# The softplus step of a selective-scan kernel: where its last sums and its product run

## The chip, the cores and the metric

The kernel runs on one core of one Trainium2 chip. The metric is device time in microseconds, from one launch to the end; the time before is the median of three runs. The engines are named as in the profile: PE is TensorE (matrix products), DVE is VectorE, ACT is ScalarE, POOL is GpSimd, SP only issues DMAs.

## The reference, cut to what matters

A model of four layers works on four images of 96 channels and 64 x 64 pixels. Layer 0 is a selective scan in four directions over 192 inner channels with 16 states each; layer 1 is a deformable convolution; layers 2 and 3 are a Fourier filter, a linear attention and two quantised feed-forward blocks. The change lies in layer 0, where the step size `delta` is a softplus:

```python
dts = jnp.einsum('bkrl,kdr->bkdl', dts, dt_w)
...
delta = jax.nn.softplus(dts + delta_bias[None, :, :, None])
...
dA = jnp.exp(d_t[..., None] * A)
h = dA * h + (d_t * u_t)[..., None] * b_t[:, :, None, :]
y = jnp.einsum('bkdn,bkn->bkd', h, c_t)
```

So for each direction, channel and pixel the kernel needs `delta` and `delta * u`, before the scan reaches that pixel.

## The kernel before, in words

**The scan** (`Layer0.scan`) is the backbone of the program. It has 1536 units (4 images, 4 directions, 4 pieces of 1024 pixels, 24 groups of 8 channels times 16 states on 128 partitions). A unit loads `delta` for its channels, each row repeated 16 times, into `da` (`fetch`, L911, a DMA issued by ScalarE); ScalarE takes the exponential (`decay`, L932, two units ahead); TensorE spreads `delta * u` over the states into the PSUM tile `db` (`inflow`, L938, one unit ahead); VectorE multiplies `db` by B in place (`enter`, L952) and runs the recurrence (`recur`, L960); GpSimd keeps the last column (L967) and multiplies by C (`weigh`, L969); TensorE sums over the states into `py` (`total`, L988), which ScalarE copies out (`settle`, L999).

**Beside the scan** two streams of other work are emitted: one makes the inputs of layer 0 image by image (`before`: normalisation, convolution at L691, and the chains below) and afterwards layers 2 and 3; the other runs what follows the scan of layer 0 and then layer 1 with its gathers (L1301, L1312, L1331, L1352). Each is a generator that yields steps, and each step says what it should take of each engine: `cost(pe=..., dve=..., act=..., pool=...)`. A planner (`Clock`, `pipe`, `Stream`) adds these up at the time of building and emits a step when its engines have room and its input is due. The order of instructions on every engine is the order of emission. The numbers in `cost` are the planner's estimates, not measurements. A step can also say how many of the three shared PSUM banks its chain holds (`holds`), and take or free a token for a buffer (`takes`, `frees`); a chain waits where a token is missing.

**The chains** (`Layer0.steps`) make `delta` and `delta * u` for 512 pixels on 128 partitions; there are 192 of them, 48 for each image, up to five at a time in `pipe`. A chain's stages are, in order:

- TensorE multiplies the projected inputs by `dt_w` into the PSUM tile `pd` (L769). ScalarE takes `ex = exp(-|pd|)` (L771, L772), `lw = ln(ex + 1)` (L774) and `w1 = ex + 1` (L775).
- VectorE takes `w1 - 1 - ex`, which is what was lost in rounding `ex + 1` (L778). GpSimd subtracts it from `lw` (L780). VectorE takes `rl = max(pd, 0) + lw`, which is `delta` (L782).
- VectorE multiplies `rl` by `u` into `ex` (L785, where the direction runs down the columns and `u` is read with a stride; L791 elsewhere). SP writes `rl` to DRAM (L794).
- ScalarE and TensorE split `ex` into three bf16 parts (L798 to L808; `minus` is minus the identity in bf16), which SP writes to DRAM (L812). `inflow` reads them back.

The tiles `lw` and `w1` exist once, `rl` and `du` twice, `ex` three times, as do the shared PSUM banks.

Of the kernel before, what the change touches and what calls it, by code (L numbers as in the profile page):

```python
# [10 lines left out]
BF16 = mybir.dt.bfloat16  # L11
# [4 lines left out]
ALU = mybir.AluOpType  # L16
# [9 lines left out]
CH = 512  # L26
# [157 lines left out]
def cost(pe=0.0, dve=0.0, act=0.0, pool=0.0, **more):  # L184
    return Step((pe, dve, act, pool), **more)


def wait(us=0.0, **more):

    return Step((0.0,) * 4, us, **more)  # L190
# [75 lines left out]
class Chain:  # L266
    def __init__(self, steps, ready):
        self.steps, self.ready = steps, ready
        self.done, self.holds, self.new, self.takes = 0, 0, True, []
        self.kind = steps.gi_code  # L270


def pipe(net, chains, width, every=0, **tiles):
# [5 lines left out]
    while True:  # L279
        if more and len(active) < width:  # L280
            steps = next(chains, None)
            if steps is None:
                more = False
            else:
                active.append(Chain(steps, clock.now()))
                continue
# [252 lines left out]
class Layer0:  # L539
# [211 lines left out]
    def steps(self, b, ks, j, us, dtw, sm, xdbl):  # L751

        net = self.net
        nc = net.nc
        cs = slice(j * CH, (j + 1) * CH)
        tk = f"{b}_{j}_" + "".join(str(k) for k in ks)
        both = len(ks) == 2

        def tile_of(name, bufs):
            return sm.tile([128, CH], F32, name=f"{name}{tk}", tag=name, bufs=bufs)  # L760

        yield wait(new=True, takes="ex lw")


        pd = net.mm(f"pd{tk}")
        for k in ks:
            q = k % 2
            o, m = (pd[64 * q : 64 * q + 64], slice(128, DI)) if both else (pd, slice(0, 128))
            nc.tensor.matmul(o, lhsT=dtw[:, k, m], rhs=xdbl[q, j], start=True, stop=True)  # L769
        ex = tile_of("ex", 3)  # L770
        nc.scalar.activation(ex, pd, AF.Abs)  # L771
        nc.scalar.activation(ex, ex, AF.Exp, scale=-1.0)  # L772
        lw, w1 = tile_of("lw", 1), tile_of("w1", 1)
        nc.scalar.activation(lw, ex, AF.Ln, bias=net.one)  # L774
        nc.scalar.activation(w1, ex, AF.Identity, bias=net.one)  # L775
        yield cost(pe=2.2 if both else 1.1, act=2.7, holds=1, takes="rl")
        rl = tile_of("rl", 2)
        nc.vector.scalar_tensor_tensor(w1, w1, -1.0, ex, ALU.add, ALU.subtract)  # L778
        yield cost(dve=0.7, holds=1)
        nc.gpsimd.tensor_sub(lw, lw, w1)  # L780
        yield cost(pool=1.3, holds=1)
        nc.vector.scalar_tensor_tensor(rl, pd, 0.0, lw, ALU.max, ALU.add)  # L782
        yield cost(dve=0.7, frees="lw")
        if not both and ks[0] % 2:
            nc.vector.tensor_mul(  # L785
                ex.rearrange("p (w h) -> p w h", h=H),
                rl.rearrange("p (w h) -> p w h", h=H),
                us[1][:, j * NR : (j + 1) * NR, :],
            )
        else:  # L790
            nc.vector.tensor_mul(ex, rl, us[2 if both else 0][:, cs])  # L791
        parts = ((0, 64, ks[0], 128), (64, 128, ks[1], 128)) if both else ((0, 128, ks[0], 0),)
        for p0, p1, k, c0 in parts:
            nc.sync.dma_start(self.de_d[b][k][c0 : c0 + p1 - p0, cs], rl[p0:p1])  # L794
        yield cost(dve=0.7, takes="du", frees="rl")

        du = sm.tile([128, 3, CH], BF16, name=f"du{tk}", tag="du", bufs=2)
        nc.scalar.copy(du[:, 0, :], ex)  # L798
        yield cost(act=0.6, new=True)
        pr = net.mm(f"pr{tk}")  # L800
        nc.tensor.matmul(pr, lhsT=net.ident, rhs=ex, start=True, stop=False)  # L801
        nc.tensor.matmul(pr, lhsT=self.minus, rhs=du[:, 0, :], start=False, stop=True)
        nc.scalar.copy(du[:, 1, :], pr)
        yield cost(pe=1.5, act=0.6, holds=1, frees="ex")
        nc.tensor.matmul(
            pr, lhsT=self.minus, rhs=du[:, 1, :], start=False, stop=True, skip_group_check=True
        )
        nc.scalar.copy(du[:, 2, :], pr)  # L808
        yield cost(pe=0.4, act=0.6)
        for p0, p1, k, c0 in parts:  # L810
            dst = self.du_d[b][k][:, c0 : c0 + p1 - p0, cs]
            nc.sync.dma_start(dst.rearrange("s c t -> c s t"), du[p0:p1])  # L812
        self.ready.update((b, k, both, j) for k in ks)
        yield wait(frees="du")
# [974 lines left out]
```

## Time and profile before

| what | value |
|---|---|
| median of three runs | 9014.61 us (9012.24 to 9038.34) |
| profiled execution, first to last instruction (span) | 8965.3 us |
| median of the runs less that span | 49.3 us (the profiled execution's own whole time is not given) |
| granted TensorE clock, mean | 0.807 |
| VectorE busy | 6689.3 us, 4995 instructions |
| TensorE busy | 6639.1 us, 31960 products |
| GpSimd busy | 5561.5 us, 4307 instructions |
| ScalarE busy | 5244.1 us, 10214 instructions |

The profile is one execution of the program, recorded by the hardware. A row of a group reads: line, engine, operation, output<-inputs by the program's names, shapes, count; then busy time in us and the mean of one in ns; then the time for which the engine stood idle just before such an instruction, and what ended that idle time. A row of a table of windows gives, for a stretch of time, the busy time of each engine with its number of instructions, the granted clock, the share of the DMA engines and the GB/s. A row of one line's view gives minimum, median and maximum in ns.

### The profile page before, as it was taken

The numbers are of one execution on the slowest core, as the hardware profiler recorded it, in microseconds if no ns is written. First come the engines' busy times: TensorE is split into PE (matmuls) and PEld (weight loads), VectorE is DVE, ScalarE is ACT, GpSimd is POOL, SyncE is SP. The second block draws the span as 40 slices with busy tenths as digits, with TensorE's granted clock in tenths as the row PEclk, the third lists the DMA queues.
The fourth block names the chain that finished last, engine by engine and source line by source line (L and its number), as shares of the span: only waits on it lengthen the run. The fifth ranks groups of instructions, "written<-read, shape, count | busy, mean of one in ns | idle before, by whom it ended". The sixth has DMA issues, their size and how long they took to land.

```text
span 8965.3 us, 97776 instructions
## 1 busy us (share of the span) xinstructions
PE 6639.1 (74%) x31960; PEld 2926.8 (33%) x31960; DVE 6689.3 (75%) x4995; ACT 5244.1 (58%) x10214; POOL 5561.5 (62%) x4307
## 2 busy tenths in 40 slices
PE   6675967687767678777667888776888777766687
PEld 2111311122222233312223554122455322454373
DVE  0498889987889987788898887898887889223414
ACT  4564656555567767755566665545666665267623
POOL 0365657666668888766688887667888876245200
PEclk8776977798778889877778888787898887867798
DMA  1476777767778888877788888667888876434120
GB/s 51 133 205 173 193 191 220 198 183 181 189 202 231 235 224 228 204 199 194 200 230 219 233 218 213 160 177 193 215 229 222 216 188 156 104 108 131 57 62 12
DMA packets 776001, 1608.49 MB, mean 179 GB/s; under 512 B 247810, under 2 KB 339358, under 8 KB 773383
## 3 DMA queue, kind: packets, MB, share of 16 engines
q10 hardware_dynamic: 244224, 843.17, 36.4%
q1 hardware_dynamic: 457542, 532.51, 22.0%
q0 software_dynamic: 73728, 226.57, 9.6%
q8 instruction: 257, 4.21, 0.2%
q14 instruction: 250, 2.04, 0.1%
HBM read 1345.62 MB, written 256.29 MB: 179 GB/s over the span
## 4 chain that ended last, share of the span: by engine, by line
PE 35%; DVE 27%; DMA 15%; ACT 10%; issue 7%; POOL 2%; SPq 2%; ACTq 1%; another core or an unknown queue 0%; DVEq 0%; POOLq 0%
DVE hh L960 13%; DVE db L952 7%; DMA du<-du 5%; PE pc L691 4%; PE py L988 4%; ACT g L1312 4%; PE ps L1331 3%; PE db L938 3%; PE f L1425 3%; DMA da<-de 2%; PE pd L1347 2%; POOL hh L969 1%; DMA bc<-bcd 1%; ACT da L932 1%; PE h L1466 1%
## 5 line engine op out<-in xcount | busy, mean ns | idle before, releaser
L969 POOL TENSOR_TENSOR hh<-hh,bc 128x1024 f32<-128x1024 f32 x1536 | 3658.6, 2384 | 351.9 <-DVE hh L960 244.2
L960 DVE TENSOR_TENSOR_SCAN hh<-da,st,db 128x1024 f32<-128x1024 f32 x1152 | 2701.1, 2345 | 229.9 <-PE py L988 86.1
L952 DVE TENSOR_TENSOR db<-db,bc 128x1024 f32<-128x1024 f32 x1536 | 1863.4, 1213 | 523.2 <-PE db L938 517.9
L932 ACT ACTIVATE da<-da,w_al 128x1024 f32<-128x1024 f32 x1536 | 1741.5, 1146 | 641.0 <-DMA da<-de 287.2
L938 PE MATMUL db<-du,rep 96*128 96x512 bf16 x3072 | 1101.2, 447 | 824.6 <-DVE hh L960 764.5
L1301 POOL DMA_INDIRECT g<-table,idx x1152 | 1151.2, 999 | 546.3 <-issue 195.7
L1312 ACT ACTIVATE g<-g,wt 128x96 f32<-128x96 f32 x4608 | 1282.6, 365 | 146.8 <-DMA du<-du 37.3
L988 PE MATMUL py<-hh,w_fold 128*32 128x512 f32 x6144 | 1055.2, 760 | 24.2 <-POOL hh L969 10.7
L960 DVE TENSOR_TENSOR_SCAN hh<-da,db 128x1024 f32<-128x1024 f32 x384 | 877.3, 2285 | 71.9 <-PE py L988 22.1
L1331 PE MATMUL ps<-w_ident,g 128*96 128x128 f32 x3744 | 682.8, 322 | 300.6 <-ACT g L1312 142.7
L938 PEld LDWEIGHTS <-rep 96*128 96x128 bf16 x3072 | 284.3, 107 | 1772.3 <-issue 1139.0
L780 POOL TENSOR_TENSOR lw<-lw,w 128x512 f32<-128x512 f32 x192 | 244.3, 1273 | 820.9 <-DVE w L778 808.7
L1331 PEld LDWEIGHTS ps<-w_ident,g 128*96 128x96 f32 x3744 | 483.2, 142 | 655.0 <-ACT g L1312 255.2
L967 POOL COPY st<-hh 128x1 f32<-128x1 f32 x1152 | 233.3, 202 | 696.0 <-DVE hh L960 637.4
L691 PE MATMUL pc<-pad,wc 96*128 96x512 f32 x1152 | 548.4, 616 | 53.4 <-DMA wc<-wc_d 46.8
L1339 ACT COPY st<-ps 96x384 f32<-96x384 f32 x384 | 180.2, 472 | 395.5 <-PE ps L1331 301.6
L801 PE MATMUL pr<-ex,w_ident 128*128 128x512 f32 x384 | 281.5, 823 | 173.0 <-DVE ex L791 89.8
L778 DVE SCALAR_TENSOR_TENSOR w<-w,ex 128x512 f32<-128x512 f32 x192 | 159.4, 830 | 285.7 <-ACT w L775 285.6
L1318 DVE TENSOR_TENSOR g<-g 128x576 f32<-128x576 f32 x96 | 72.9, 759 | 390.0 <-ACT g L1312 360.5
L691 PEld LDWEIGHTS pc<-pad,wc 96*128 96x128 f32 x1152 | 217.1, 195 | 336.4 <-issue 305.3
L988 PEld LDWEIGHTS py<-hh,w_fold 128*32 128x32 f32 x6144 | 153.9, 122 | 511.0 <-issue 384.4
L769 PE MATMUL pd<-xd,w_dtw 103*64 103x512 f32 (+1 forms) x512 | 267.1, 800 | 66.5 <-DVE rl L782 27.5
(249 smaller groups left out, 8899.5 us busy)
## 6 DMA issues: line engine op xcount, KB each, us to landing
da<-de ACTq DMA_DIRECT2D x1536, 512.0 KB
du<-du SPq DMA_DIRECT2D x512, 192.0 KB
bc<-bcd SPq DMA_DIRECT2D x128, 512.0 KB
du<-du SPq DMA_DIRECT2D x128, 384.0 KB
y<-yb SPq DMA_DIRECT2D x384, 128.0 KB
de<-rl SPq DMA_DIRECT2D x128, 256.0 KB
m<-in_dft SPq DMA_DIRECT2D x128, 256.0 KB
ad<-y ACTq DMA_DIRECT2D x192, 128.0 KB
```

What stands on the lines that cost most here:

```text
L691: nc.tensor.matmul(pp, lhsT=wc[:, q, g * 128 : (g + 1) * 128], rhs=pad[:, r0 + dy : r0 + dy + NR, dx : dx + W], start=(q == 0), stop=(q == 8),
L801: nc.tensor.matmul(pr, lhsT=net.ident, rhs=ex, start=True, stop=False)
L932: self.net.nc.scalar.activation(u.da, u.da, AF.Exp, scale=self.al[:, a : a + 1])
L938: self.net.nc.tensor.matmul(db[:, h, :], lhsT=self.rep[:96, u.s % 4, :], rhs=u.du[u.s // 4][:, h * CH : (h + 1) * CH], start=True, stop=True,)
L952: self.net.nc.vector.tensor_mul(u.db, u.db, u.bc[:, 0, :])
L960: nc.vector.tensor_tensor_scan(u.along(u.hh), u.along(u.da), u.along(u.db), first, ALU.mult, ALU.add)
L969: self.net.nc.gpsimd.tensor_mul(u.hh, u.hh, u.bc[:, 1, :])
L988: nc.tensor.matmul(py[p0 : p0 + 32], lhsT=self.fold[:, u.i, :], rhs=hc[:, h * CH : (h + 1) * CH], start=u.sums["add"] is None and u.i == 0 ...
L1301: nc.gpsimd.indirect_dma_start(out=g[:, k, :], out_offset=None, in_=self.tables[b % 2], in_offset=bass.IndirectOffsetOnAxis(ap=idx[:, n : ...
L1312: nc.scalar.activation(pixel, pixel, AF.Identity, scale=wt[:, n, c : c + 1])
L1331: nc.tensor.matmul(pt[:, k, :], lhsT=g[:, k, c * C : (c + 1) * C], rhs=net.ident, is_transpose=True, start=(c == 0), stop=(c == corners - 1),)
L1425: nc.tensor.matmul(pt[64 * part : 64 * part + 64, c, :], lhsT=d[:, :, c0 + c], rhs=matrix[:, 64 * part : 64 * part + 64], start=True, stop ...
```

## The change

The subtraction of what was lost in rounding leaves GpSimd. VectorE writes it as a bf16 tile `lost`, forms `max(pd, 0) + lw` in place in the PSUM tile, TensorE adds minus `lost` to it there, and ScalarE copies the finished `delta` to `rl`. The product with `u` goes from VectorE to GpSimd. The planner's costs and the tokens of the steps are changed with it: the chain has one step fewer, `rl` is taken one step later, and the bank is held for two steps where it was held for three.

```diff
-        yield cost(pe=2.2 if both else 1.1, act=2.7, holds=1, takes="rl")
+        yield cost(pe=2.2 if both else 1.1, act=2.7, holds=1)
+
+        lost = sm.tile([128, CH], BF16, name=f"lost{tk}", tag="lost", bufs=1)
+        nc.vector.scalar_tensor_tensor(lost, w1, -1.0, ex, ALU.add, ALU.subtract)
+        nc.vector.scalar_tensor_tensor(pd, pd, 0.0, lw, ALU.max, ALU.add)
+        yield cost(dve=1.5, holds=1, takes="rl")
         rl = tile_of("rl", 2)
-        nc.vector.scalar_tensor_tensor(w1, w1, -1.0, ex, ALU.add, ALU.subtract)
-        yield cost(dve=0.7, holds=1)
-        nc.gpsimd.tensor_sub(lw, lw, w1)
-        yield cost(pool=1.3, holds=1)
-        nc.vector.scalar_tensor_tensor(rl, pd, 0.0, lw, ALU.max, ALU.add)
-        yield cost(dve=0.7, frees="lw")
+        nc.tensor.matmul(pd, lhsT=self.minus, rhs=lost, start=False, stop=True, skip_group_check=True)
+        nc.scalar.copy(rl, pd)
+        yield cost(pe=0.4, act=0.6, frees="lw")
         if not both and ks[0] % 2:
-            nc.vector.tensor_mul(
+            nc.gpsimd.tensor_mul(
                 ex.rearrange("p (w h) -> p w h", h=H),
                 rl.rearrange("p (w h) -> p w h", h=H),
                 us[1][:, j * NR : (j + 1) * NR, :],
             )
         else:
-            nc.vector.tensor_mul(ex, rl, us[2 if both else 0][:, cs])
+            nc.gpsimd.tensor_mul(ex, rl, us[2 if both else 0][:, cs])
         parts = ((0, 64, ks[0], 128), (64, 128, ks[1], 128)) if both else ((0, 128, ks[0], 0),)
         for p0, p1, k, c0 in parts:
             nc.sync.dma_start(self.de_d[b][k][c0 : c0 + p1 - p0, cs], rl[p0:p1])
-        yield cost(dve=0.7, takes="du", frees="rl")
+        yield cost(pool=1.3, takes="du", frees="rl")
```

## The prediction

> **What bounds the kernel now.** I read the page first: no engine is busy for more than 75% of the span, but the slices show that the average hides two stages.
>
> ```profile
> PE 6639.1 (74%) x31960; PEld 2926.8 (33%) x31960; DVE 6689.3 (75%) x4995; ACT 5244.1 (58%) x10214; POOL 5561.5 (62%) x4307
> ...
> DVE  0498889987889987788898887898887889223414
> ```
>
> VectorE is at eight or nine tenths from slice 3 to slice 34 (about 350 to 7640 us, the scan) and low before and after. Next, the groups: what the scan needs of each engine for one of its 1536 units.
>
> ```profile
> L969 POOL TENSOR_TENSOR hh<-hh,bc 128x1024 f32<-128x1024 f32 x1536 | 3658.6, 2384 | 351.9 <-DVE hh L960 244.2
> L960 DVE TENSOR_TENSOR_SCAN hh<-da,st,db 128x1024 f32<-128x1024 f32 x1152 | 2701.1, 2345 | 229.9 <-PE py L988 86.1
> L952 DVE TENSOR_TENSOR db<-db,bc 128x1024 f32<-128x1024 f32 x1536 | 1863.4, 1213 | 523.2 <-PE db L938 517.9
> L780 POOL TENSOR_TENSOR lw<-lw,w 128x512 f32<-128x512 f32 x192 | 244.3, 1273 | 820.9 <-DVE w L778 808.7
> ```
>
> A unit costs VectorE 2.33 + 1.21 = 3.54 us and GpSimd 2.38 + 0.2 = 2.6 us; everything else on VectorE comes on top. The changed code (`steps`, 192 chains) runs in four waves, one for each image. I took a table of windows over them, then one stretch without chains:
>
> ```profile
> core 0: us, PE busy (x) PEld busy (x) DVE busy (x) ACT busy (x) POOL busy (x), PEclk, DMA share, GB/s
> 354.20:715.00 360.80, 254.34 (x708) 67.18 (x708) 323.73 (x254) 239.18 (x351) 233.69 (x177) 0.78 0.68 195
> 1157.00:1680.00 523.00, 362.84 (x1151) 91.51 (x1149) 494.13 (x362) 329.26 (x469) 339.61 (x229) 0.77 0.78 211
> 2201.00:3160.00 959.00, 671.80 (x2599) 237.27 (x2601) 857.36 (x589) 613.31 (x1193) 713.48 (x549) 0.77 0.79 213
> 3781.00:4745.00 964.00, 682.29 (x2393) 217.20 (x2394) 840.76 (x597) 569.79 (x1001) 678.75 (x512) 0.77 0.77 205
> ...
> 4860.00:5200.00 340.00, 277.90 (x2165) 172.35 (x2163) 288.50 (x182) 213.52 (x495) 290.15 (x230) 0.89 0.89 230
> ```
>
> In the waves VectorE is 87 to 94% busy, all others 59 to 74%. The same windows of the scan line alone hold 71, 110, 200 and 190 units: 5.08, 4.75, 4.80 and 5.07 us each. The last window has 80 units, 4.25 us each, with VectorE at 85%: that pace is my floor, set there by GpSimd and DMA. So the waves are bound by VectorE, and work taken off it there shortens the scan.
>
> Then the rows of the chain itself (by form, and the lines' minimum, median, maximum):
>
> ```profile
> L785 DVE TENSOR_TENSOR ex<-rl,xa 128x512 f32<-128x512 f32 x64 | 109.7, 1714 | 2.2
> L791 DVE TENSOR_TENSOR ex<-rl,xa 128x512 f32<-128x512 f32 x64 | 77.5, 1211 | 1.8
> L791 DVE TENSOR_TENSOR ex<-rl,xc 128x512 f32<-128x512 f32 x64 | 63.8, 998 | 2.1
> L782 DVE SCALAR_TENSOR_TENSOR rl<-pd,lw 128x512 f32<-128x512 f32 x192 | 130.3, 679 | 27.6 <-POOL lw L780 21.8 <-DMA de<-rl 5.8
> L805 PE MATMUL pr<-du,minus 128*128 128x512 bf16 x192 | 86.9, 453 | 30.2 <-ACT du L803 30.1
> L999 ACT COPY yb<-py 128x512 f32<-128x512 f32 x192 | 110.2, 574 | 117.4 <-DVE hh L960 37.4 <-DMA du<-du 20.8 <-PE py L988 10.5
> ```
>
> ```profile
> L791 DVE TENSOR_TENSOR ex<-rl,xa x64: 674/692/5339, 305.1 to 4740.5; 128x512 f32<-128x512 f32 x64
> ...
> L782 DVE SCALAR_TENSOR_TENSOR rl<-pd,lw x192: 655/680/694, 279.3 to 4739.8; 128x512 f32<-128x512 f32 x192
> ```
>
> The reader is to see that the product takes 0.69 us at the median but 1.2 us in the mean, while the step before it, with one operand in PSUM, never exceeds 0.694.
>
> **What the skill says.** The Trainium skill, "SBUF — State Buffer", Who interferes with whom: a VectorE instruction with two SBUF inputs contends with a GpSimd one that reads SBUF, and the later one waits for the whole of the other. The trace agrees: see L791 against L782. "GPSIMD Engine Reference", Elementwise: two-input work is about half as fast there; L780's 1273 ns against 680 agrees. "PSUM — Partial Sum Buffer", the four PSUM rules: GpSimd cannot touch PSUM, hence the ScalarE copy before the moved product; and VectorE's write leaves the bits by which a product without a start flag adds, so the product adds to what VectorE left. No run yet shows that last part.
>
> **The change part by part** (192 chains).
> VectorE: the products L785 and L791 go: 109.7 + 77.5 + 63.8 = 251.0 us. By the windows 7.6 of this lies before the first unit, where VectorE idles and nothing is won; 243.4 lies inside the scan. L778 becomes `lost`, same two f32 inputs, bf16 out: 0.83 us as now. It may inherit lock waits that the product met: from −0.15 (none left) to +0.4 us (what L791 loses on average), −29 to +77 us; I take 0, since its operands and place are as before. L782 writes in place in PSUM: L952 does so in 1.213 us for 1024, which less 512 columns at 0.96 GHz ("VectorE: DVE Perf Modes", Specifications; an estimate) leaves 0.68, as now; bounds ±10 us.
> GpSimd: 192 subtractions go (244.3 us), 192 products come: 128 plain at 1.27, 64 strided at 1.52 (L1052 reads a strided operand in 1518 ns at the median): 260 us. The 16 us more hide under VectorE (GpSimd is at 65 to 74% in the waves); uncovered, they would cost 16.
> TensorE: one bf16 product and its weight load, 192 x (0.45 + 0.11) = 108 us. ScalarE: 192 copies at 0.574 = 110 us. Over the waves' 2807 us that is 4% each: TensorE from 70 to 74%, ScalarE from 62 to 66%, plus its 571 issues of `da` loads at 0.52 us, 11%. Both stay under VectorE.
> Queues: the DMAs of `rl` (L794) stay as many, on SP, in the same place; they now wait for ScalarE's copy in place of VectorE. On TensorE the new product waits for two VectorE instructions; behind it stand the `db` products of the next units. On ScalarE the copy waits for that product; behind it stand the exponentials of `da`, issued two units ahead (VectorE waits for them only 24.8 us in all). On GpSimd the product waits for the copy; behind it stands `hh`, which TensorE needs three units later. The order is planned so that a step is emitted once its input is due, so I expect waits, but short ones.
> The planner sees 1.5 us of VectorE work for a chain where it saw 2.1, one step fewer, and `lw` free without the GpSimd stage between, so chains may follow one another faster and the stream of later stages comes forward.
>
> Sum: without new waits the waves run at 4.54, 4.18, 4.45 and 4.71 us a unit; only the second falls under the floor, (4.25 − 4.18) x 110 = 8 us lost. VectorE now waits in the waves for `db` 57 + 32 + 55 = 144 us; with TensorE fuller and one more wait in its queue I add a third, 45 us. 243 − 8 − 45 = 190 us. The tail after the scan: two strands end 69 us apart (the last `xo` of image 3 at 8444, the last FFN row of image 2 at 8513, then image 3 alone): if the later one comes forward, up to 69 us more; I take 0. Span 8965 − 190 = 8775; the median of the runs lies 49.3 us above this span, so about 8825.
>
> **The rivals.** *Slower: TensorE becomes the bound.* Now TensorE idles before L801 for VectorE's product 193.4 + 96.2 us (with the weight loads), 128 times, 2.26 us each. From GpSimd that product comes 0.58 us later, and up to one `hh` (2.38) after that; with the new wait in front, each chain could hold the in-order queue, `db` comes late and VectorE idles. It decides from 235/192 = 1.22 us of new idle for each chain; at 1.7 us, 326 − 235 = 91 us slower, 9106. For it: VectorE's largest wait is already for `db`, 518 us. Against: TensorE waits for the scan before `db` 764 us, so it has slack of its own.
> *No change: another pace.* If GpSimd or DMA set the waves' pace as they set the floor, what VectorE saves turns into its idle time: 9015. Against: waves one and two run slower than the floor with DMA at 0.68 and 0.78.
> *It doesn't do what it says:* the added operations are all real; what may differ is the emitted order, every later stage being planned anew. That is worth tens of us either way and is in the range.
>
> **Numbers.** VectorE relief 0.68 (8825; its own range 8690 to 8960), no change 0.10, TensorE 0.22. Range 8690 to 9060. Within 0.3% (27 us) is about what a measurement of this kernel can't tell from no change.
>
> **What would show it.** Right: VectorE about 250 us less busy and 4803 instructions; waves at 4.2 to 4.7 us a unit with VectorE still near 90%; scan ending near 7450. Wrong: VectorE's wait for `db` well above 518 us, TensorE's or its weight loads' waits on the new `pd` product or on `ex` above 400 us (TensorE); equal scan end with more VectorE idle and no such waits (other pace); `lost` at 1.2 us (the lock wait only moved).

## The result, and the profile after

The changed kernel took **8932.76 us** in the median (8907.99 to 8966.76) against 9009.08 (8959.19 to 9038.34) for the kernel before on the same chip. The ratio of the runs, 0.9931 [0.9916, 0.9947] (95% interval), is 62 us (48 to 76); the two medians lie 76 us apart. The direction was right; the gain was about a third of the 190 us that were forecast.

The profiled execution took 8943.91 us as a whole with a span of 8942.1, so 1.8 us lie around a span. The span of before that the prediction used therefore belonged to an execution of 8967.1 us, 42 below that kernel's median. The two spans lie only 23 us apart where the medians lie 76 apart: what these traces say of *where* the time went is good to some 50 us, and the ratios carry the verdicts below. Where in the program the 62 us were won, the traces don't show.

The page of the changed kernel, busy time and slices:

```profile
PE 6647.8 (74%) x32152; PEld 2943.2 (33%) x32152; DVE 6549.9 (73%) x4803; ACT 5334.2 (60%) x10406; POOL 5560.8 (62%) x4307
...
DVE  0488889886888877788888787998887978323314
```

VectorE has the 4803 instructions that were foretold, but it is only 139.4 us less busy (6689.3 − 6549.9), not 250. The page of before has this row for the subtraction:

```profile
L778 DVE SCALAR_TENSOR_TENSOR w<-w,ex 128x512 f32<-128x512 f32 x192 | 159.4, 830 | 285.7 <-ACT w L775 285.6
```

The groups of the changed kernel's page say where the rest is:

```profile
L971 POOL TENSOR_TENSOR hh<-hh,bc 128x1024 f32<-128x1024 f32 x1536 | 3638.2, 2371 | 366.3 <-DVE hh L962 257.2
L962 DVE TENSOR_TENSOR_SCAN hh<-da,st,db 128x1024 f32<-128x1024 f32 x1152 | 2700.9, 2345 | 267.0 <-PE py L990 108.2
L954 DVE TENSOR_TENSOR db<-db,bc 128x1024 f32<-128x1024 f32 x1536 | 1864.2, 1214 | 608.0 <-PE db L940 592.6
...
L779 DVE SCALAR_TENSOR_TENSOR lost<-w,ex 128x512 bf16<-128x512 f32 x192 | 252.1, 1313 | 319.1 <-ACT w L775 318.8
L787 POOL TENSOR_TENSOR ex<-rl,xa 128x512 f32<-128x512 f32 x64 | 98.6, 1540 | 551.9 <-ACT rl L784 549.2
```

`lost` (L779) takes 1313 ns in the mean where the same subtraction took 830 before: 192 x 0.483 = 93 us. And VectorE's wait for `db` rose from 517.9 to 592.6 us. The views of the chain's lines (minimum, median and maximum in ns):

```profile
L779 DVE SCALAR_TENSOR_TENSOR lost<-w,ex x192: 665/836/5655, 277.6 to 4663.1; 128x512 bf16<-128x512 f32 x192
...
L780 DVE SCALAR_TENSOR_TENSOR pd<-pd,lw x192: 681/686/695, 278.2 to 4663.7; 128x512 f32<-128x512 f32 x192
...
L783 PE MATMUL pd<-lost,minus x192: 376/380/634, 279.0 to 4670.4; 128*128 128x512 bf16 x192
```

The step with one operand in PSUM (`pd`, L780) lies between 681 and 695 ns in all 192 cases. The one with two operands in SBUF (`lost`, L779) starts at 665 and goes to 5655. Before, 26 of the 192 subtractions took over 0.9 us (the trace, instruction by instruction); now 94 do. Each of these 26 and 94 ends 0.54 to 0.56 us after a GpSimd instruction ended. One of the long ones, in the changed kernel's timeline (start and duration in us, engine, line):

```profile
4457.64 4.69 POOL L971 TENSOR_TENSOR hh<-hh,bc 128x1024 f32<-128x1024 f32 x2
...
4458.29 4.60 DVE L779 SCALAR_TENSOR_TENSOR lost<-w,ex 128x512 bf16<-128x512 f32 x1
...
4462.81 0.69 DVE L780 SCALAR_TENSOR_TENSOR pd<-pd,lw 128x512 f32<-128x512 f32 x1
```

GpSimd runs two multiplications back to back until 4462.33; `lost`, which starts while the first runs, ends at 4462.89, 0.56 us after the second. It counts as busy all that time. It is a wait of the kind that the prediction read off L791, now on another instruction.

The same windows as before:

```profile
core 0: us, PE busy (x) PEld busy (x) DVE busy (x) ACT busy (x) POOL busy (x), PEclk, DMA share, GB/s
354.20:715.00 360.80, 258.08 (x730) 69.26 (x731) 298.14 (x212) 256.87 (x385) 221.73 (x173) 0.80 0.68 193
1157.00:1680.00 523.00, 368.72 (x1211) 95.38 (x1204) 471.36 (x319) 346.82 (x503) 339.95 (x230) 0.80 0.79 213
2201.00:3160.00 959.00, 676.36 (x2675) 241.19 (x2668) 825.42 (x547) 637.66 (x1249) 723.17 (x557) 0.79 0.81 217
3781.00:4745.00 964.00, 683.38 (x2456) 210.75 (x2455) 821.36 (x560) 595.75 (x1032) 684.23 (x515) 0.79 0.80 210
```

VectorE went from 87–94% to 83–90%, and the windows hold 70, 115, 200 and 196 units where they held 71, 110, 200 and 190: 581 for 571. VectorE got room and filled only part of it. The granted clock in these windows is 0.79 to 0.80, where it was 0.77 to 0.78. From the first scan instruction to the last the scan takes 7288 us here and 7268 in a second trace (`e9_after_again`); in two traces of the kernel before it took 7283 and 7303. After the first two waves, with the same 96 chains done, VectorE has spent 62 us less beside the scan than before (326 to 264 us), and yet the first 384 units take as long as before, 1805 us.

### The profile page after: what moved, and what is told of

Same layout as the page of the kernel before. It is cut to its first block, busy times and chain, and to the rows that moved or that the text cites. A ratio compares the mean times of both kernels' runs of the same rounds, so it can differ in the third digit from the quotient of the medians.

```text
span 8942.1 us, 98509 instructions
## 1 busy us (share of the span) xinstructions
PE 6647.8 (74%) x32152; PEld 2943.2 (33%) x32152; DVE 6549.9 (73%) x4803; ACT 5334.2 (60%) x10406; POOL 5560.8 (62%) x4307
## 4 chain that ended last, share of the span: by engine, by line
PE 34%; DVE 23%; DMA 17%; ACT 11%; issue 8%; POOL 3%; ACTq 1%; SPq 1%; another core or an unknown queue 0%; DVEq 0%; POOLq 0%
DVE hh L962 12%; DVE db L954 6%; DMA du<-du 5%; PE pc L691 4%; ACT g L1314 4%; PE py L990 4%; PE ps L1333 3%; PE db L940 3%; PE f L1427 3%; DMA da<-de 3%; PE pd L1349 2%; ACT da L934 2%; POOL hh L971 1%; PE py L985 1%; DMA bc<-bcd 1%
## 5 line engine op out<-in xcount | busy, mean ns | idle before, releaser
L954 DVE TENSOR_TENSOR db<-db,bc 128x1024 f32<-128x1024 f32 x1536 | 1864.2, 1214 | 608.0 <-PE db L940 592.6
L940 PE MATMUL db<-du,rep 96*128 96x512 bf16 x3072 | 1074.9, 437 | 819.3 <-DVE hh L962 775.2
L990 PE MATMUL py<-hh,w_fold 128*32 128x512 f32 x6144 | 1034.9, 746 | 17.3 <-ACT yb L1001 5.9
L779 DVE SCALAR_TENSOR_TENSOR lost<-w,ex 128x512 bf16<-128x512 f32 x192 | 252.1, 1313 | 319.1 <-ACT w L775 318.8
L787 POOL TENSOR_TENSOR ex<-rl,xa 128x512 f32<-128x512 f32 x64 | 98.6, 1540 | 551.9 <-ACT rl L784 549.2
L1349 PE MATMUL pd<-st,wdc 96*128 96x256 f32 x1152 | 309.9, 417 | 4.4 <-ACT st L1341 4.4
L803 PE MATMUL pr<-ex,w_ident 128*128 128x512 f32 x384 | 270.8, 795 | 44.5 <-POOL ex L787 17.3
```

The costliest lines, as they stand in the source:

```text
L940: self.net.nc.tensor.matmul(db[:, h, :], lhsT=self.rep[:96, u.s % 4, :], rhs=u.du[u.s // 4][:, h * CH : (h + 1) * CH], start=True, stop=True,)
L954: self.net.nc.vector.tensor_mul(u.db, u.db, u.bc[:, 0, :])
L990: nc.tensor.matmul(py[p0 : p0 + 32], lhsT=self.fold[:, u.i, :], rhs=hc[:, h * CH : (h + 1) * CH], start=u.sums["add"] is None and u.i == 0 ...
L1349: nc.tensor.matmul(po, lhsT=wdc[:, k, :], rhs=st[:, k, :], start=(k == 0), stop=(k == 8))
```

## The experiments

Theory: VectorE's busy time in the waves is worth time, and the wait at the port that VectorE shares with GpSimd moved from the product to `lost`. Rivals: TensorE became the bound; another pace (GpSimd, DMA) holds the scan; the order of emission, planned anew, makes the difference. A further one, the granted clock, is taken up behind the table. The ratios below are to the kernel before, on the chip of that run.

**The product made short, before's code otherwise** (`e1_product_short`):

```diff
-            nc.vector.tensor_mul(ex.rearrange(...), rl.rearrange(...), us[1][:, j * NR : (j + 1) * NR, :])
+            nc.vector.tensor_mul(ex[:, :8], rl[:, :8], us[1][:, j * NR, :8])
...
-            nc.vector.tensor_mul(ex, rl, us[2 if both else 0][:, cs])
+            nc.vector.tensor_mul(ex[:, :8], rl[:, :8], us[2 if both else 0][:, j * CH : j * CH + 8])
```

> The kernel before with its order unchanged, the product of delta and u on VectorE cut to 8 of 512 columns (the rest of ex stays as it was, so delta times u is left out). Theory V (VectorE's time sets the pace of the waves): VectorE is about 200 to 240 us less busy and the time falls by 130 to 240 us, ratio 0.974 to 0.986. Theory O (the pace comes from the order in which the engines must serve one another, TensorE above all): VectorE's idle time grows by most of what it saves, the time falls by less than 70 us, ratio above 0.992. Theory L (the wait for the shared port only moves): the remaining step with two SBUF inputs, L778, grows from 0.83 to about 1.2 us; under V alone it stays at 0.83.

Measured: 0.9922 [0.9895, 0.9948]. `delta * u` is left out here but for these columns. The views of the two product lines of this kernel:

```profile
L785 DVE TENSOR_TENSOR ex<-rl,xa x64: 158/173/4461, 283.2 to 4594.3; 128x8 f32<-128x8 f32 x64
...
L787 DVE TENSOR_TENSOR ex<-rl,xc x64: 153/168/3024, 285.3 to 4615.9; 128x8 f32<-128x8 f32 x64
L787 DVE TENSOR_TENSOR ex<-rl,xa x64: 151/168/4849, 304.2 to 4677.4; 128x8 f32<-128x8 f32 x64
```

Eight columns take 0.17 us at the median, yet the three groups hold 50.1 + 48.3 + 32.3 = 130.7 us, 0.68 us each: three quarters of that is waiting. Of the 251 us that the prediction took off VectorE, about 100 were not work at all. L778 kept its 0.82 us here: the short product still does the waiting.

**`lost` with an operand in PSUM, the change otherwise** (`e2_lost_no_lock`; `lost` is made of `pd` and `w1` here):

```diff
-        nc.vector.scalar_tensor_tensor(lost, w1, -1.0, ex, ALU.add, ALU.subtract)
+        nc.vector.scalar_tensor_tensor(lost, pd, -1.0, w1, ALU.add, ALU.subtract)
```

> The changed kernel with its order unchanged, but the step lost reads pd in PSUM in place of ex, so that it has one SBUF input (what was lost in rounding is then not what is subtracted: delta is wrong by this). Theory L: the step falls from 1.31 to 0.68 us, VectorE is about 120 us less busy. Theory V: the time falls by 60 to 120 us below the changed kernel, ratio to before 0.978 to 0.986. Theory O: it stays within 30 us of the changed kernel, ratio 0.989 to 0.995.

Measured: 0.9843 [0.9817, 0.9868]. Its groups by form:

```profile
L780 DVE SCALAR_TENSOR_TENSOR pd<-pd,lw 128x512 f32<-128x512 f32 x192 | 132.4, 690 | 0.0
L779 DVE SCALAR_TENSOR_TENSOR lost<-pd,w 128x512 bf16<-128x512 f32 x192 | 130.8, 681 | 326.1 <-ACT w L775 325.9
```

Only the operands differ, one of them now in PSUM, and 1313 ns become 681: the extra 121 us were the wait at the port. The end moves by 0.9 points (about 80 us) with them. What is taken off is then not the rounding, so the result is not that of the change.

**The product on GpSimd alone** (`e3_product_pool`, before with `nc.gpsimd.tensor_mul` at L785 and L791 and the step's cost as `pool=1.3`) and **the sums in PSUM alone** (`e4_psum_only`, the change with `nc.vector.tensor_mul` and `dve=0.7`):

> The kernel before with only the product moved to GpSimd (and its planned cost with it); the step size is finished as before. VectorE 251 us less busy in the product, GpSimd 260 us more. Theory V: ratio 0.985 to 0.993, with L778 at about 1.2 us (L). Theory O: 0.995 to 1.005, the two GpSimd stages in each chain giving back what VectorE saves.

> The changed kernel with the product back on VectorE (and its planned cost with it): only the finish in PSUM is left of the change. Theory V: VectorE is as busy as before, so ratio 0.997 to 1.003. Theory O: if the gain came from the chain's shorter way (no GpSimd stage between two VectorE steps, lw free sooner, the stream of later stages further ahead at the scan's end), the ratio is that of the whole change, 0.990 to 0.995.

Measured: 1.0033 [1.002, 1.0045] and 1.0098 [1.0073, 1.0123]. Neither half helps. In both the subtraction waits, by form (`e3`, then `e4`):

```profile
L778 DVE SCALAR_TENSOR_TENSOR w<-w,ex 128x512 f32<-128x512 f32 x192 | 221.0, 1151 | 310.4 <-ACT w L775 310.1
```

```profile
L779 DVE SCALAR_TENSOR_TENSOR lost<-w,ex 128x512 bf16<-128x512 f32 x192 | 282.2, 1470 | 279.3 <-ACT w L775 279.2
```

The first is the unchanged subtraction at 1151 ns. The scan shortened to 7184 us, but the chain passes GpSimd twice, the last product of the last wave ended at 4922 us where it was 4742, and the stream behind came late: 7224 TensorE products were left after the scan where before left 6916, and the tail took 1472 us, not 1328. In the second, product and `lost` both wait (1470 ns for `lost`, 1.47 to 1.73 us for the products), and VectorE is 131 us *busier* than before.

Set side by side with before (830 ns, 26 of 192 over 0.9 us) and the change (1313 ns, 94), the two halves narrow down why `lost` waits. Either half alone brings the wait: the product off VectorE (`e3`, 1151 ns, 83 of 192), or the subtraction off GpSimd with the product still on VectorE (`e4`, 1470 ns, 102). So `lost` does not wait only because the product is gone. The trace of before shows what else may have kept its subtraction short: GpSimd stood idle until L778 was done in 159 of the 192 chains, 808.7 us in all, since its own step L780 needs the result. A GpSimd instruction other than an indirect DMA was running at the start of L778 in 30 chains, at the start of `lost` in 104. That this is the reason in `e4` and in the change is argued; `e3` keeps L780 and waits all the same, with 192 products more on GpSimd.

**The kernel before once more** (`e5_before_again`) and **the changed kernel once more** (`e9_after_again`), for a second trace of each:

> The kernel before, unchanged, for a second trace: the first trace of before is of an execution of 8967 us, 42 us under the median of its runs, so the two traces that are compared differ by less than the two medians. Theory H (about half of the time taken off VectorE reaches the end): a more usual execution shows its scan ending 20 to 50 us later than 7637, with the same busy time on VectorE, so that the change's scan is shorter after all. Otherwise the scan ends at 7637 plus or minus 15 and the change gained only in the tail.

> The changed kernel, unchanged, for a second trace on the chip of its companions. Two traces of before have scans of 7283 and 7304 us and tails of 1328 and 1287 us (the tail differs from chip to chip); the one trace of the changed kernel has 7288 and 1294. Theory Q (the scan hardly shortens, since what VectorE saves is paid back on the way through TensorE and ScalarE): the scan is again 7270 to 7310. Otherwise, if that trace was an unlucky one, 7200 to 7260.

8947.71 us beside a median of 8948.48; and 0.9919 [0.9894, 0.9944], VectorE 6557.8 us, `lost` 1368 ns in the mean. The scans of these traces are among those given above.

**`lost` on GpSimd** (`e6_lost_pool`, with one more ScalarE step so that a plain subtraction does):

```diff
+        nc.scalar.activation(w1, w1, AF.Identity, bias=net.neg)
...
-        nc.vector.scalar_tensor_tensor(lost, w1, -1.0, ex, ALU.add, ALU.subtract)
+        nc.gpsimd.tensor_sub(lost, w1, ex)
```

> The changed kernel with its order unchanged, but lost made on GpSimd: ScalarE takes 1 from w1 first, then GpSimd subtracts ex (the result is the same). VectorE loses its last step with two SBUF inputs in the chains: 252 us less busy than in the changed kernel. Theory H: half of this reaches the end, 110 to 140 us below the changed kernel, ratio to before 0.976 to 0.980. Rival W (the chains' way through GpSimd's queue is what counts, as where the product alone was moved): the waves end later than 4660 us, the tail grows, ratio 0.988 to 1.000.

Measured: 1.0006 [0.9991, 1.0021], with VectorE 375 us less busy. Its waits say what became of them:

```profile
DVE db L957 <- PE db L943: 771.0, 313, 23.1
...
DVE hh L965 <- PE py L993: 184.1, 134, 7.0
```

VectorE is free of the wait at the port in the chains and waits for TensorE instead. GpSimd carries 5772.6 us here, 211 more than before.

**Dose on VectorE** (`e7_vector_dose`: `e2` with both VectorE steps on 8 columns, which the product L783 then reads over and over) and **dose on TensorE** (`e8_tensor_dose`: `e2` without the two products L803 of a chain):

```diff
-        nc.vector.scalar_tensor_tensor(pd, pd, 0.0, lw, ALU.max, ALU.add)
+        nc.vector.scalar_tensor_tensor(pd[:, :8], pd[:, :8], 0.0, lw[:, :8], ALU.max, ALU.add)
```

```diff
-        nc.tensor.matmul(pr, lhsT=net.ident, rhs=ex, start=True, stop=False)
-        nc.tensor.matmul(pr, lhsT=self.minus, rhs=du[:, 0, :], start=False, stop=True)
+        nc.tensor.matmul(pr, lhsT=self.minus, rhs=du[:, 0, :], start=True, stop=True)
```

> e2_lost_no_lock with its order unchanged and both VectorE steps of a chain cut to 8 of 512 columns (delta is left out for the rest): VectorE about 200 us less busy than in e2. Theory H (a constant share of about 0.55): 110 us below e2, ratio 0.970 to 0.974. Theory F (VectorE is no longer what bounds the waves by then): less than 50 us below e2, ratio 0.979 to 0.985. Theory V (VectorE alone bounds the waves): 180 to 200 us below e2, 0.962 to 0.965.

> e2_lost_no_lock with its order unchanged and the two f32 products of ident and ex taken out of each chain (delta times u then misses this part): TensorE about 270 us less busy. If TensorE shares the bound with VectorE, since what VectorE waits for is db from TensorE, the time falls by 80 to 150 us below e2, ratio 0.968 to 0.976. If only VectorE and its lock count, it stays within 30 us of e2, ratio 0.981 to 0.988.

Measured: 0.9776 [0.9752, 0.98] and 0.9868 [0.9844, 0.9891]. VectorE's 182 us less (6418.2 to 6236.5) gave another 0.7 points. TensorE's 384 products fewer gave nothing that can be told from `e2`. But the dose was small: they had taken 258.5 us of TensorE in `e2`, and TensorE is only 97 us less busy (6617.4 to 6520.4), because the other products took longer, at a granted clock of 0.796 where `e2` has 0.814:

```profile
L990 PE MATMUL py<-hh,w_fold 128*32 128x512 f32 x6144 | 1023.9, 740 | 24.6 <-ACT yb L1001 8.3
```

```profile
L989 PE MATMUL py<-hh,w_fold 128*32 128x512 f32 x6144 | 1057.3, 761 | 17.6 <-POOL hh L970 6.2
```

The first is `e2`, the second `e8`. So this run does not settle whether TensorE shares the bound.

**The added TensorE product taken out** (`e10_no_minus`: L783 goes), **the changed kernel with another figure for the planner** (`e11_plan`: `dve=2.1` where it has 1.5), and **three VectorE steps without a wait at the port** (`e12_three_steps`: `ex` in PSUM, `delta` finished by VectorE):

```diff
-        nc.vector.scalar_tensor_tensor(lost, w1, -1.0, ex, ALU.add, ALU.subtract)
-        nc.vector.scalar_tensor_tensor(pd, pd, 0.0, lw, ALU.max, ALU.add)
...
-        nc.tensor.matmul(pd, lhsT=self.minus, rhs=lost, start=False, stop=True, skip_group_check=True)
-        nc.scalar.copy(rl, pd)
+        nc.vector.scalar_tensor_tensor(pd, w1, -1.0, pd, ALU.add, ALU.subtract)
+        nc.vector.scalar_tensor_tensor(pd, pd, -1.0, lw, ALU.mult, ALU.add)
+        nc.vector.tensor_add(rl, pd, up)
```

> The changed kernel with its order unchanged, without the minus-ones product (delta then lacks the correction for rounding, lost is still made): ScalarE's copy follows VectorE directly. Theory Q, TensorE's place in it: the product waits 122 us for VectorE in TensorE's in-order queue and holds db behind it; without it the scan falls by 50 to 80 us, ratio to before 0.984 to 0.988. Rival: the wait is hidden, as a product more or less on TensorE was in e8; within 20 us of the changed kernel, ratio 0.991 to 0.995.

> The changed kernel with only the planner's figure for the VectorE step of a chain set from 1.5 to 2.1 us, near the 2.0 it takes with the lock wait; the instructions are the same, their order changes. If the too small figure made the planner put too much beside a unit: ratio 0.985 to 0.990. If the figure does not matter: within 30 us of the changed kernel, 0.990 to 0.997.

> A version made from the findings: ex is kept in PSUM, ScalarE sets max(pd, 0) aside, and VectorE finishes delta in three steps that have one SBUF input each, straight into rl; the product stays on GpSimd, and neither TensorE nor a copy by ScalarE stands between. The result is the same. Three steps at 0.68 are 2.04 us of VectorE for a chain, as the changed kernel's two with the lock wait (2.00). By VectorE's time alone (theory H): equal to the changed kernel, ratio 0.991 to 0.996. Theory Q: the scan is 50 to 80 us shorter on top, ratio 0.983 to 0.988.

Measured: 0.9895 [0.9867, 0.9922], 1.0014 [0.9996, 1.0031] and 1.0152 [1.0124, 1.018]. The product is worth some 20 us between the medians (8905.28 and 8925.31 in `e9`, on the same chip), and the intervals of the two ratios overlap. `e11` has the change's instructions in another order and loses all of the gain: its scan is no longer (7236 us), but 7008 TensorE products are left for the tail where the change leaves 6896, and the tail takes 1426 us, not 1297. One figure of the planner thus moves the end by as much as the whole gain. In `e12` the three steps take 686 to 699 ns each in the mean, with no wait, and the last product still ended at 5010 us where the change's ended at 4688: here too the chains came late. In `e3`, `e11` and `e12` 40 of the 64 pieces of feed-forward work came after the scan, in the change and before 32. Such pieces run partly on other engines by then, so VectorE has 47 or 48 instructions more in these three (4850 in `e11`): their VectorE figures are not the chains' alone.

**`delta` made directly** (`e13_direct`: VectorE writes `rl`; no product L783, no copy L784; `lost` is made and not used) and **without `lost` and `w1`** (`e14_no_correction`):

```diff
-        nc.vector.scalar_tensor_tensor(pd, pd, 0.0, lw, ALU.max, ALU.add)
+        rl = tile_of("rl", 3)
+        nc.vector.scalar_tensor_tensor(rl, pd, 0.0, lw, ALU.max, ALU.add)
...
-        nc.tensor.matmul(pd, lhsT=self.minus, rhs=lost, start=False, stop=True, skip_group_check=True)
-        nc.scalar.copy(rl, pd)
```

> The changed kernel with its order unchanged, but VectorE writes delta straight into rl (a third buffer of it), without the minus-ones product and without ScalarE's copy; lost is still made and not used (delta then lacks the correction for rounding). VectorE's steps and their lock wait stay. e10 without the product alone was 0.9895 against 0.9919 for the changed kernel. Theory Q (the way through both engines pays back what VectorE saves): the scan falls by another 30 to 40 us to about 7225, ratio 0.984 to 0.987. Rival R (the rest of it lies in the order that the planner makes from the new figures, which this kernel keeps): ratio 0.988 to 0.991, scan 7245 to 7265.

> e13_direct without lost and without w1 (the correction for rounding is left out altogether): VectorE loses its last step with two SBUF inputs in the chains, about 252 us, and ScalarE 135 us. Theory H (0.3 to 0.6 of the time taken off VectorE reaches the end, less as more is taken): 80 to 140 us below e13, ratio 0.970 to 0.978. If the lock wait moves on to some other step: less than 50 us below e13.

Measured: 0.9917 [0.9894, 0.994] and 0.9745 [0.9717, 0.9773], 8697.16 us. The way through PSUM, TensorE and ScalarE costs nothing that can be told (0.9917 with it gone, 0.9931 and 0.9919 with it). The single VectorE step that waits at the port, with its ScalarE step, costs 1.7 points.

**The order alone** (`e15_direct_old_order`: the instructions of `e13` under the steps and costs of before, with two `rl` tiles where `e13` has three; `e16_change_old_order`: the whole change under them):

```diff
-        yield cost(dve=1.5, holds=1, takes="rl")
-        rl = tile_of("rl", 2)
+        yield cost(dve=0.7, holds=1)
+        yield cost(pool=1.3, holds=1)
...
-        yield cost(pe=0.4, act=0.6, frees="lw")
+        yield cost(dve=0.7, frees="lw")
```

> The same instructions in a chain as e13_direct, but in the order and with the planner's figures of the kernel before: lost on VectorE (made and not used, the correction for rounding is left out), delta straight into rl, the product on GpSimd. e13 has 0.9917 and a scan of 7253 us. Theory R (the new order pays back what VectorE saves): with the old order the scan falls to 7200 to 7235 (before less about half of some 145 us), ratio 0.983 to 0.988. Otherwise the old order gives no more than the new, ratio 0.989 to 0.994.

> All instructions of the change (the result is the same as the changed kernel's) in the order and with the planner's figures of the kernel before, which does not know of the product on TensorE and the copy on ScalarE. If the new order is what pays back and the way costs some 20 us: ratio 0.985 to 0.990, ahead of the changed kernel's 0.9919 to 0.9931. If the unplanned wait of TensorE for VectorE holds db behind it at each chain: 0.993 to 1.000.

Measured: 0.9977 [0.9965, 0.999] and 1.0285 [1.0268, 1.0303]. That the new order itself was the cost, as one theory had it, falls: the old order is worse with either set of instructions. TensorE's waits in `e16`, then in the changed kernel (total, times, longest):

```profile
PE db L940 <- DVE hh L962: 638.1, 337, 12.9
PE pd L783 <- DVE pd L782: 430.7, 148, 16.5
```

```profile
PE db L940 <- DVE hh L962: 775.2, 424, 21.1
...
PE pd L783 <- DVE pd L780: 122.1, 79, 6.2
```

Where the planner does not know of the product and the copy, TensorE stands at its queue's head for 431 us in place of 122, the `db` products behind it are late (VectorE waits 666.9 us for them, the trace's waits say), and 62 us of gain become 257 us of loss. This is the slower rival of the prediction, held off in the change by its new steps, tokens and cost figures.

## What VectorE's time was worth

Ratios against VectorE's busy time on the page, less than before's 6689.3 us; the gain is (1 − ratio) x 9000 us. The last column is explained below:

| run | VectorE less busy, us | gain, us | gain for each us | gain at equal clock, us (estimate) |
|---|---|---|---|---|
| the change (twice) | 139, 132 | 62, 73 | 0.45, 0.55 | (no clock of before), 21 |
| `e1`, product short | 129 | 70 | 0.55 | 41 |
| `e2`, `lost` without the wait | 271 | 141 | 0.52 | 72 |
| `e4`, sums in PSUM only | −131 | −88 | 0.67 | −79 |
| `e7`, `e8` | 453, 271 | 202, 119 | 0.45, 0.44 | 107, 163 |
| `e10`, `e13`, `e14` | 144, 143, 384 | 95, 75, 230 | 0.66, 0.52, 0.60 | 61, 57, 161 |
| `e3`, `e11`, `e15` | 180, 136, 173 | −30, −13, 21 | −0.16, −0.09, 0.12 | −32, −42, 9 |
| `e6`, `e12`, `e16` | 375, 118, 156 | −5, −137, −257 | none | −38, −94, −223 |

Ten runs, from 131 us more to 453 us less, lie between 0.44 and 0.67: about half of what VectorE sheds reaches the end. Six runs don't lie there, and they were set apart only once their results were known. `e3`, `e11` and `e12` have more work left after the scan. In `e6`, `e12` and `e16` the scan is no shorter (7320, 7320 and 7523 us). Of `e6` and `e15` the reason stays open: `e6`'s chains ended no later than the change's (4684 and 4688 us), and `e15`'s scan took 7243 us and its tail 1355, with no more products in it (6916) than before.

**The granted clock is a rival that these runs don't remove.** Executions of one kernel on one chip differ in it, and in time with it: over the 276 executions whose clock is on record, taken within each kernel and chip, the time falls by 5.0 us for each 0.001 of clock (correlation −0.70). For the 21 executions of the kernel before beside `e9` it is 5.6 us (−0.87). `e9`'s six executions have 0.812 in the mean and those 21 have 0.8025; at 5.0 us this alone would be 46 of the 67 us between their mean times. The last column is the difference of the mean times with that part taken out. What is left still grows with VectorE's relief, but in those of the ten that have relief, `e8` aside, it is 0.16 to 0.42 us for each us. In `e8`, which has less TensorE work and a lower clock, more is left (163 us) than in `e2` (72), so TensorE's work may well count too. The clock does not decide alone: `e6` has 0.811 and gains nothing. Whether the change itself brings the higher clock, so that the whole gain is its own, or the clock came with something else, no run here shows.

Where the other half goes is seen in part, why is only argued. VectorE's idle time within the scan grew from 1033 and 1051 us to 1168 and 1139; of it, the waits for `db` (those over 0.15 us) grew from 504 and 511 to 575 and 553. These products in turn wait for VectorE's scan (764.5 us before, 775.2 in the change), which frees one of only two `db` tiles: a ring, whose round need not get shorter when chain steps are taken from between. A third `db` tile was not tried.

## Why the prediction was right and wrong, step by step

- **What bounds the waves: right, too strong.** VectorE's load sets time (`e2`, `e7`); that TensorE's does not is not shown (`e8`). And "work taken off it there shortens the scan" was taken at 235/243; the rate is about half, or less. The slices read as "eight or nine tenths" also hold sevens.
- **"`lost` ... I take 0, since its operands and place are as before": the step that failed first.** It measured +93 us, beyond the upper bound of 77. Its operands and place were as before, but not what GpSimd does at that moment. That it waits, and for GpSimd's instructions, is shown, and `e3` and `e4` show that either half of the change is enough; how each half brings it is argued. The prediction had named the sign for this ("`lost` at 1.2 us"), and it showed 1.31. So 139 us came free, not 251.
- **"I add a third, 45 us" of new waits: the step that failed next.** 190 of 243 us is a rate of 0.78; measured, 62 of 139, or 0.45. At the forecast's own rate the freed 139 us would have given 109. VectorE's wait for `db` rose by 75 us in all (517.9 to 592.6), and part of the 62 us may be the clock's. The sum had a slip as well: the 57 us were read over 354 to 1700 us, with the stretch between the waves; the first two waves alone have 0.8 and 12.7, so a third would have been 33 us, not 45. The rival "another pace" was thus half true, and its cause stays open.
- **GpSimd's 260 us: right.** 98.6 for the strided products and 164.0 for the others (1281 ns in the mean). The page's total stayed (5561.5 to 5560.8).
- **TensorE +108, ScalarE +110, hidden: right within what can be told.** The product and its weight load took 90.6 + 20.8 = 111 us, the copy 113 us; `e13` without both is no faster by a clear margin.
- **VectorE's step in place in PSUM, 0.68: right** (686 ns). The product without a start flag adds to what VectorE wrote, as the Trainium skill, "PSUM — Partial Sum Buffer", The four PSUM rules, let one expect: the result still holds `delta`, so it was not replaced, and other contents of `lost` (`e2`) change the result, so they arrive.
- **The TensorE rival: not by its signs in the change.** 122 us of wait on the new product where 400 was the sign, and before L803 the wait for `ex` fell from 193.4 + 96.2 to 49.8 + 25.8 us. `e16` shows the rival alive.
- **"The median lies 49.3 us above this span": misread.** It was the distance of one execution from the median. The forecast was formed against the median all the same. The measured time lies in the range 8690 to 9060, but that range was wide enough to hold a loss as well.
- **Scan end near 7450, waves at 4.54, 4.18, 4.45 and 4.71 us a unit: wrong.** The scan ended at 7648 and 7629, and the windows run at 5.15, 4.55, 4.80 and 4.92. **Tail at 0: within what the traces can tell** (1294 and 1297 us, before 1328 and 1287).

## What to carry to other kernels

A busy row whose mean lies well above its median holds a wait, and a wait at a shared port is not removed for good with the instruction that shows it: another VectorE step with two SBUF operands can meet GpSimd in its place, so credit only the median for such an instruction (here 128 x 0.69 + 64 x 1.08 = 158 us; 139 came free). Look also at which engine stood idle for which step: the subtraction that GpSimd mostly waited for was held up in 26 chains of 192, and in 102 once GpSimd no longer waited for it (`e4`). Move one operand into PSUM and the wait goes altogether (`e2`, `e12`). Price a busy engine in a ring of dependent steps at less than its busy time, here about half, and less with the clock taken out, and change the planner's figures together with the instructions (`e16`), trying more than one: a figure nearer to what the step takes lost the whole gain (`e11`). When two kernels differ by as little as here, compare their granted clocks before giving the whole difference to the change.

## What the runs showed that was not expected

- A VectorE step of 8 columns and two SBUF operands took 0.68 us in the mean, four times its median of 0.17, and up to 4.8 us: three quarters of such a step's time is the wait for GpSimd.
- One VectorE step was held across *two* GpSimd multiplications in a row (4.60 us in the timeline above, 5.66 at most), though the second had not begun when the step started; 8 of the 94 long ones were. "SBUF — State Buffer", Who interferes with whom, in the Trainium skill has an exclusive lock on the shared ports; that the one who waits can lose it twice is what this trace adds.
- The granted TensorE clock of the changed kernel was higher (0.813 and 0.814 against 0.807 and 0.806 in the traces), and within one kernel a higher clock goes with a shorter time, as told above.
- Two ways to keep the correction without VectorE's wait at the port (`e6`, `e12`) did not win, and the fastest kernel, `e14`, is without the correction. Among the kernels that compute the whole, none measured here beats the changed one.
